# A graph layer on one core: a fixed order for VectorE's instructions in a step, and three buffers for the node columns' comparisons

## Chip, cores, metric

The kernel runs on one core of one Trainium2 chip. The metric is the device time of one execution in microseconds (us). TensorE is called PE in the profile, VectorE DVE, ScalarE ACT, GpSimd POOL; SP only issues DMAs.

## What is computed

A layer of a graph network with a residual connection and a layer norm, on 12500 nodes of 128 features and 400000 edges, sorted by target:

```python
Xs = X[src]
msg = where(edge_type == 0, Xs @ W_data.T + b_data, Xs @ W_control.T + b_control)
agg = segment_sum(msg, dst, num_segments=12500)
h = relu(agg + X @ W_self.T + b_self)
out = layernorm(x + h)
```

## The kernel before

**Groups, windows and pairs.** The 3125 chunks of 128 edges are 25 groups of 125 chunks. Since the edges are sorted by target, a chunk touches a narrow window of targets. Of each 25 chunks, 5 go one way (p) and 20 another (e). For a p chunk, GpSimd gathers the rows of the source nodes by an indirect DMA into `msg` (L825), and TensorE adds them up: `msg` is multiplied by a 0/1 matrix `psel` into a window of sums (L757). For the 20 e chunks, a *pair* (g, i), there is no gather. All x rows lie in SBUF (`x3`, in three bf16 parts). The edges of the pair are ordered by source block, and TensorE picks the source rows with a 0/1 matrix `pick` (L926, output `got`); ScalarE copies `got` to `emsg` (L940); TensorE multiplies `emsg` by a 0/1 matrix `esel` into sums (L757). There are 107 pairs and so 107 *steps*, each of which runs about 15 us. In a step w, pair w is picked, pair w+2 is ranked, pair w+3 is begun; p chunks are gathered and added on the side.

**The chain of one pair on VectorE.** `block_matrix`, `fours` and `same_lane` begin a pair: O compares each edge's source block with the 100 blocks (L533, 128x2000); `fours` adds up O's columns in groups of ten and of five (L614, L615); `same_lane` compares the edges of one lane with each other (L604). `before` multiplies by a triangular matrix on TensorE (L624). `ranks` then gives each edge its place: `ahead` (L632, reads PSUM), the product O times ahead (L636), two folds that halve the width (L641, 128x1200 and 128x600), `found` (a reduction, L643), `rank` (L645). `rank_matrix` compares ranks with 32 columns (`rm`, L533, 128x640) and multiplies with the values (`rv`, L676). `over` looks for edges whose rank is over 32 (`key` L649, `top` L653, `over_n` L660, `bits`). `put` on TensorE places the values (L688), ScalarE copies them to `cell` (L696), two DMAs on SP write them to memory and read them back to all partitions (`pick<-there`, L701), and VectorE turns them into the pick matrix (L743, in place). L709 transposes the cells on TensorE.

**The node columns' comparisons.** `choose` in `picked` builds `esel` in three parts per step: 10, 9 and 6 columns (L533 with 128x1760, 128x1584, 128x1056), traced in the turns t = 0, 1 and 3. They share two buffers.

**Spare columns.** Edges over rank 32 go through extra columns: `own_before` (L552 on TensorE, L558 `om_all` on VectorE), `own_turn` (L564), and one gather per two pairs (`both`, L901), which ScalarE copies to `last` (L988).

**Preparing a group.** `prep(g)` has four parts (`begin`, `rows`, `turn`, `then`), placed in steps at 0.15, 0.4, 0.65 and, a step later, at 0.1. `rows` works on VectorE (L494 to L499), `turn` transposes on TensorE (L504), `then` splits the indices (L511, L512, L515).

**What sets the order.** In each step, `merged` sorts lists of (position between 0 and 1, function) and calls them in that order. That is the order of tracing, not yet that of the engines: a planner then orders each engine's queue once, when the program is built, by the place in the trace and by its own estimate of when an instruction is ready. On the chip each queue runs in that order. `tc.issue_after(ins)` ties what is traced inside it behind `ins` on the same engine. `placed[0]` is the last `rv` that has been traced; `behind`, `pick_matrix` and `later` (which wraps the parts of `prep`) tie to it. The planner is free with everything else, O among it. `evenly` spreads a list over a step. `paced` gives each gather a wait for an instruction of TensorE, so that gathers follow the steps.

The steps of the loop that hold these lists, with the positions of before: `before` in turn t = 1, `ranks` 0.31, `rank_matrix` 0.35, `rows` 0.4, `begin_slots(w + 3)` 0.55, `pick_matrix(w + 1)` 0.6, `over` 0.75.

Of the kernel before, what the change touches and what calls it, by code (L numbers as in the profile page):

```python
# [8 lines left out]
FP = mybir.dt.float32  # L9
# [197 lines left out]
def short_path(ctx, tc, const, ident, eps, wT, brow, bad, x, src, dst, etype, ws, bs, out):  # L207
# [320 lines left out]

    def select(sel, col, code2):

        rows, n, width = sel.shape
        shape = [rows, n, width // 2, 2]
        nc.vector.tensor_tensor(  # L533
            sel.rearrange("p n (w t) -> p n w t", t=2),
            col[:rows].rearrange("p (o w t) -> p o w t", o=1, t=2).to_broadcast(shape),
            code2.rearrange("p n (o t) -> p n o t", o=1).to_broadcast(shape),
            op=OP.is_equal,
        )
        return sel

# [44 lines left out]
    def give_slots(w):  # L585
# [4 lines left out]

        def behind():
            return tc.issue_after(placed[0].ins) if w > 1 else ExitStack()

        def block_matrix():
            O = s["held"] = two.tile([P, EC * NCELL], BF, name="O")
            s["O"] = O.rearrange("p (c j) -> p c j", j=NCELL)
            select(s["O"], cell_cols[w % 2], blk2)

        def same_lane():
# [3 lines left out]
            with behind():  # L603
                nc.vector.tensor_tensor(  # L604
                    eq.rearrange("p a (b t) -> p a b t", t=2),
                    blk2.rearrange("p a (o t) -> p a o t", o=1).to_broadcast(shape),
                    run,
                    op=OP.is_equal,
                )
        def fours():  # L610
            s["prod"] = big.tile([P, EC, NCELL + EC], BF, name="prod")
            h = s["few"] = s["prod"][:, :, :NCELL]
            with behind():
                nc.vector.tensor_add(h[:, :2 * CQ], s["O"][:, :2 * CQ], s["O"][:, 2 * CQ:])  # L614
            nc.vector.tensor_add(h[:, 2 * CQ:3 * CQ], h[:, :CQ], h[:, CQ:2 * CQ])  # L615

# [11 lines left out]

        def ranks():
            ahead = two.tile([P, NCELL], BF, name="ahead")  # L630
            with nc.allow_low_precision(reason="whole numbers; those over 256 need not be exact"):
                nc.vector.tensor_reduce(  # L632
                    ahead, s["ahead"][:, :2 * NCELL].rearrange("p (k j) -> p j k", k=2), AX.X, OP.add
                )
            prod = s["prod"]
            nc.vector.tensor_tensor(  # L636
                prod[:, :, :NCELL], s["O"], ahead.rearrange("p (o j) -> p o j", o=1).to_broadcast([P, EC, NCELL]),
                op=OP.mult,
            )
            for h in ((NCELL + EC) // 2, (NCELL + EC) // 4):  # L640
                nc.vector.tensor_add(prod[:, :, :h], prod[:, :, :h], prod[:, :, h:2 * h])  # L641
            found = two.tile([P, EC], FP, name="found")
            nc.vector.tensor_reduce(found, prod[:, :, :h], AX.X, OP.add)  # L643
            rank = s["rank"] = two.tile([P, EC, 2], BF, name="rank")
            nc.vector.tensor_copy(rank, found.rearrange("p (c o) -> p c o", o=1).to_broadcast([P, EC, 2]))  # L645

        def over():
            key = two.tile([P, EC], FP, name="key")
            nc.vector.scalar_tensor_tensor(key, s["rank"][:, :, 0], CAP - 0.5, pk, op0=OP.is_ge, op1=OP.mult)  # L649
# [3 lines left out]
            nc.vector.max(both["top"][:, w % 2, :], key)  # L653
            if w % 2 or w == pairs - 1:
                n = w % 2 + 1
                top = both["top"][:, :n]
                full = two.tile([P, 2, 8], FP, name="full")[:, :n]
                nc.vector.tensor_scalar(full, top, 0.0, None, op0=OP.is_gt)
                with nc.allow_low_precision(reason="a whole number up to 8"):
                    nc.vector.tensor_reduce(over_n[:, w + 1 - n:w + 1], full, AX.X, OP.add)  # L660
# [11 lines left out]
        def rank_matrix():  # L672
            rm = select(big.tile([P, EC, CAP], BF, name="rm"), rank_col, s["rank"])
            rv = s["rv"] = two.tile([P, EC, 2, CAP], BF, name="rv")
            shape = [P, EC, 2, CAP // 2, 2]
            placed[:] = [nc.vector.tensor_tensor(  # L676
                rv.rearrange("p c v (r t) -> p c v r t", t=2),
                rm.rearrange("p c (o r t) -> p c o r t", o=1, t=2).to_broadcast(shape),
                vals2.rearrange("p c v (o t) -> p c v o t", o=1).to_broadcast(shape),
                op=OP.mult,  # L680
            )]

# [51 lines left out]
        return s, [(0.58, block_matrix), (0.6, fours), (0.66, same_lane)], [  # L734
            (0.1, before), (0.31, ranks), (0.35, rank_matrix), (0.75, over),
        ]

    def pick_matrix(w):

        def half(a, b):  # L740
            t = slots[w]["pick"][:, a:b].rearrange("p j r -> p (j r)")
            with tc.issue_after(placed[0].ins):
                nc.vector.tensor_scalar(t, t, lane_f, None, op0=OP.is_equal)  # L743
        return [(0.6, lambda: half(0, NCELL))]

# [99 lines left out]
    def choose(g, i):  # L845

        sel = sp.tile([P, CHUNKS, 2 * PW], BF, name="psel")
        chosen[g, i] = select(sel, near_col, codes["p", g][1][:, i * CHUNKS:(i + 1) * CHUNKS])

# [56 lines left out]
    def picked(w, tiled, ending, before):  # L906
# [7 lines left out]

        def choose(q0, n):

            sel = select(sp.tile([P, 10, 2 * EW], BF, name="esel")[:, :n], code_col, slots[w]["code"][:, q0:q0 + n])
            for k in range(n):
                s["sel"][q0 + k] = sel[:, k]

        lead = 0 if w % 2 else 2
# [30 lines left out]
        def unit(t):  # L952
# [46 lines left out]

        return evenly([lambda t=t: unit(t) for t in range(turns)]), end  # L1000

# [80 lines left out]

    begun = {}

    def last_spares():
# [13 lines left out]
    def check_all():  # L1099
# [23 lines left out]
        nc.vector.tensor_copy(bad, one_i)  # L1123

    def begin_slots(w):
        slots[w], a, b = give_slots(w)
        begun[w] = b
        return [u for _, u in a]

    def all_slots(w):  # L1130
        units = begin_slots(w) + [u for _, u in begun.pop(w)]
        units += [u for t in sorted(slots[w]["tiled"]) for u in slots[w]["tiled"][t]]
# [44 lines left out]
    for w in range(pairs):  # L1177
# [8 lines left out]
        if i == 3 and g + 2 < NG:  # L1186
            load(g + 2)
        tiled, begin = {}, []
        if w + 2 < pairs:
            tiled, begin = slots[w + 2]["tiled"], begun.pop(w + 2)  # L1190
        elif w + 2 == pairs:
            tiled, begin = last_spares()
        if w + 3 < pairs:
# [5 lines left out]
        units, ending = picked(w, tiled, ending, begin.pop(0)[1] if begin else None)  # L1199
# [161 lines left out]
```

## Time and profile before

| what | value |
|---|---|
| median of 3 runs | 1719.61 us (1719.46 to 1721.19) |
| the profiled execution | 1721.01 us |
| its span, first to last instruction | 1719.3 us |
| granted clock of TensorE | 0.994 |
| gathers, L825 and L901 | 985 of 1.234 us and 54 of 1.226 us |

The page gives busy time by engine; the table by stretches the same for chosen parts of the span; the list of waits who waited for whom, with total us, times, longest. In a timeline each line has start, duration, engine, line, operation, out<-in and shape, and in brackets the idle time before it and who ended that.

### The profile page before, as it was taken

How to read it: one execution, taken by the hardware profiler on the slowest of the kernel's cores; microseconds unless marked ns; L12 is line 12 of the kernel's file. 1: busy time of each engine (PE TensorE's matmuls, PEld its weight loads, DVE VectorE, ACT ScalarE, POOL GpSimd, SP SyncE). 2: the span in 40 equal slices, each digit the busy share in tenths (PEclk: the TensorE clock that was granted, in tenths of full speed). 3: DMA queues.
4: the chain of work that ended last, by engine and by line, in shares of the span. 5: the costliest groups of instructions: out<-in, count | busy, mean ns of one | idle time of the engine just before them, and what ended most of it. 6: DMA issues, size and time to landing. Idle time of an engine off the chain costs nothing.

```text
span 1719.3 us, 68641 instructions
## 1 busy us (share of the span) xinstructions
PE 1568.1 (91%) x28525; PEld 1241.5 (72%) x28525; DVE 1529.0 (89%) x3630; ACT 1243.3 (72%) x2198; POOL 1286.8 (75%) x1061
## 2 busy tenths in 40 slices
PE   0599999999999999999899999999999999999997
PEld 0377777777777777777677777777777777777776
DVE  6899899998998989999799899999999899999983
ACT  5777677776777667777576777676777676777675
POOL 0288878888788888888788777777788787777872
PEclk9999999999999999999999999999999999999999
DMA  7844454545444454444445554545544445544442
GB/s 195 280 149 133 126 160 124 147 147 152 134 139 142 139 148 135 140 150 129 144 122 150 160 155 136 152 130 152 150 144 138 135 128 159 155 140 129 138 128 59
DMA packets 148973, 248.30 MB, mean 144 GB/s; under 512 B 35937, under 2 KB 115260, under 8 KB 148652
## 3 DMA queue, kind: packets, MB, share of 16 engines
q1 hardware_dynamic: 85994, 134.45, 23.6%
q0 software_dynamic: 50032, 102.98, 22.2%
q10 hardware_dynamic: 12626, 6.40, 1.4%
q8 instruction: 225, 3.69, 0.9%
q14 instruction: 96, 0.79, 0.1%
HBM read 226.24 MB, written 17.50 MB: 142 GB/s over the span
## 4 chain that ended last, share of the span: by engine, by line
DVE 40%; PE 38%; issue 8%; ACT 5%; DMA 4%; DVEq 1%; POOL 0%; SPq 0%; ACTq 0%; POOLq 0%
PE sums L757 16%; PE got L926 12%; DVE esel L533 5%; DVE prod L641 5%; DVE prod L636 4%; DVE rv L676 3%; DVE pick L743 3%; DVE found L643 3%; PE side L1045 3%; ACT emsg L940 2%; DVE prod L614 2%; PE side L624 2%; DMA both<-rows,idx 2%; DVE psel L533 2%; PE side L688 2%
## 5 line engine op out<-in xcount | busy, mean ns | idle before, releaser
L825 POOL DMA_INDIRECT msg<-rows,idx_g x985 | 1215.5, 1234 | 309.7 <-issue 143.8
L940 ACT CAST emsg<-got 128x768 bf16<-128x768 f32 (+1 forms) x1070 | 949.0, 931 | 296.9 <-PE got L926 277.8
L757 PE MATMUL sums<-esel,emsg 128*128 128x176 bf16 x7704 | 686.6, 240 | 3.4 <-DVE acc L814 2.9
L757 PEld LDWEIGHTS <-emsg 128*128 128x128 bf16 x7704 | 569.5, 98 | 106.1 <-issue 98.8
L926 PE MATMUL got<-x,pick 128*32 128x384 bf16 x10486 | 569.1, 330 | 17.9 <-ACT emsg L940 8.8
L926 PEld LDWEIGHTS <-pick 128*32 128x32 bf16 x10486 | 240.4, 96 | 143.8 <-issue 19.9
L533 DVE TENSOR_TENSOR esel<-code_col,code 128x1760 bf16<-128x1760 bf16 x321 | 292.9, 913 | 11.8 <-PE sums L757 8.8
L757 PE MATMUL sums<-psel,msg 128*128 128x48 bf16 x2955 | 167.2, 184 | 11.8 <-DVE acc L814 9.0
L757 PEld LDWEIGHTS <-msg 128*128 128x128 bf16 x2955 | 138.6, 97 | 21.2 <-issue 16.4
L641 DVE TENSOR_TENSOR prod<-prod 128x1200 bf16<-128x1200 bf16 x214 | 134.0, 626 | 7.2 <-issue 1.1
L533 DVE TENSOR_TENSOR O<-cell_col,blk 128x2000 bf16<-128x2000 bf16 x107 | 128.0, 1197 | 7.1 <-ACT blk L439 4.3
L636 DVE TENSOR_TENSOR prod<-O,ahead 128x2000 bf16<-128x2000 bf16 x107 | 128.3, 1200 | 4.5 <-DVE ahead L632 1.9
L743 DVE TENSOR_SCALAR pick<-pick,lane_f 128x3200 bf16<-128x3200 bf16 x107 | 112.9, 1055 | 0.1
L901 POOL DMA_INDIRECT both<-rows,idx x54 | 66.2, 1226 | 54.4 <-ACT emsg L940 41.8
L688 PE MATMUL side<-rv,O 128*128 128x64 bf16 x2140 | 83.4, 195 | 25.0 <-DVE rv L676 22.1
L533 DVE TENSOR_TENSOR psel<-near_col,near 128x1200 bf16<-128x1200 bf16 x125 | 96.7, 773 | 9.7 <-issue 8.7
L814 DVE TENSOR_TENSOR acc<-acc,sums 128x176 f32 (+2 forms) x232 | 66.8, 288 | 42.1 <-PE sums L757 41.3
L688 PEld LDWEIGHTS <-O 128*128 128x128 bf16 x2140 | 79.0, 100 | 27.2 <-DVE rv L676 22.3
L676 DVE TENSOR_TENSOR rv<-rm,vals 128x1280 bf16<-128x1280 bf16 x107 | 87.9, 822 | 3.3 <-DVE key L649 1.4
L643 DVE TENSOR_REDUCE found<-prod 128x20 f32<-128x600 bf16 x107 | 82.9, 775 | 3.2 <-DVE prod L641 0.4
L614 DVE TENSOR_TENSOR prod<-O 128x1000 bf16<-128x1000 bf16 x107 | 72.0, 673 | 0.0
L624 PEld LDWEIGHTS <-ltri 128*128 128x128 bf16 x1284 | 40.4, 96 | 40.0 <-issue 38.5
(196 smaller groups left out, 1544.6 us busy)
## 6 DMA issues: line engine op xcount, KB each, us to landing
pick<-there SPq DMA_DIRECT2D x106, 800.0 KB
msg<-rows,idx_g POOLq DMA_INDIRECT x985
acc<-acc_start SPq DMA_DIRECT2D x23, 640.0 KB
rows<-x SPq DMA_DIRECT2D x6, 1344.0 KB
xs<-in_x_dram SPq DMA_DIRECT2D x99, 62.5 KB
out_dram<-h SPq DMA_DIRECT2D x99, 62.5 KB
xt<-in_x_dram ACTq DMA_DIRECT2D x6, 896.0 KB
cnt<-cnt_start SPq DMA_DIRECT2D x22, 160.0 KB
```

Source lines behind the costliest of these rows:

```text
L533: nc.vector.tensor_tensor(sel.rearrange("p n (w t) -> p n w t", t=2), col[:rows].rearrange("p (o w t) -> p o w t", o=1, t=2).to_broadcast( ...
L614: nc.vector.tensor_add(h[:, :2 * CQ], s["O"][:, :2 * CQ], s["O"][:, 2 * CQ:])
L636: nc.vector.tensor_tensor(prod[:, :, :NCELL], s["O"], ahead.rearrange("p (o j) -> p o j", o=1).to_broadcast([P, EC, NCELL]), op=OP.mult,)
L641: nc.vector.tensor_add(prod[:, :, :h], prod[:, :, :h], prod[:, :, h:2 * h])
L643: nc.vector.tensor_reduce(found, prod[:, :, :h], AX.X, OP.add)
L676: placed[:] = [nc.vector.tensor_tensor(rv.rearrange("p c v (r t) -> p c v r t", t=2), rm.rearrange("p c (o r t) -> p c o r t", o=1, t=2).t ...
L688: nc.tensor.matmul(s["rk"][:m, :2 * CAP], s["held"][:, c * NCELL:c * NCELL + m], s["rv"][:, c].rearrange("p v r -> p (v r)"), start=(c == ...
L743: nc.vector.tensor_scalar(t, t, lane_f, None, op0=OP.is_equal)
L757: last = nc.tensor.matmul(out, msg[:, j * D:(j + 1) * D], sel, start=(start and j == 0), stop=stop, skip_group_check=True)
L825: return nc.gpsimd.indirect_dma_start(out=msg, out_offset=None, in_=rows3[:, :], in_offset=bass.IndirectOffsetOnAxis(ap=codes["p", g][0][: ...
L926: last = nc.tensor.matmul(ps[CAP * a:CAP * (a + 1), :], slots[w]["pick"][:, a * NQ + q, :], x3[:, 4 * q + a - a0].rearrange("p j d -> p (j ...
L940: s["out"] = nc.scalar.copy(msg[:, :n], ps[:, :n, :3 * D])
```

## The change

A step's instructions on VectorE are cut into single functions, and 16 of them are put into a list, `order`, each tied behind the one before it by `issue_after` (`in_turn`). The tie starts anew in each step. The order is: second comparison of the node columns, ahead, product, first fold, third comparison, second fold, found, `same` of pair w+3, rank, rank matrix, key, values (rv), pick matrix of pair w+1, O of pair w+3, its tens, its fives. What is not in the list stays free. `over` moves from 0.75 to 0.58 and holds `key` no longer. `esel` gets three buffers, and its second and third comparison leave the turns 1 and 3 of `picked`. `begin_slots(w + 3)` at 0.503 only makes the functions. Before the loop, pick matrix 0 and the begin of pair 2 are tied behind the rv of pair 1, O included.

```diff
+    def after(ins):
+        return tc.issue_after(ins.ins) if ins is not None else ExitStack()
...
-            sel = select(sp.tile([P, 10, 2 * EW], BF, name="esel")[:, :n], code_col, slots[w]["code"][:, q0:q0 + n])
+            sel = sp.tile([P, 10, 2 * EW], BF, name="esel", bufs=3)[:, :n]
+            sel, ins = select(sel, code_col, slots[w]["code"][:, q0:q0 + n], prev)
...
-            if t == 1:
-                choose(10, 9)
-            if t == 3:
-                choose(19, NQ - 19)
...
+    def in_turn(named, prev=None):
+
+        last = [prev]
+
+        def unit(f):
+            last[0] = f(last[0])
+
+        return [lambda f=f: unit(f) for f in named]
...
-    merged(pick_matrix(0))
-    for u in begin_slots(2):
+    pick_matrix(0, placed[0])
+    for u in in_turn(begin_slots(2), placed[0]):
         u()
...
-            tiled, begin = slots[w + 2]["tiled"], begun.pop(w + 2)
+            tiled, first, chain = slots[w + 2]["tiled"], slots[w + 2]["before"], slots[w + 2]["chain"]
+            begin = [(0.58, slots[w + 2]["over"])]
...
-            more += [(0.55, lambda: [u() for u in begin_slots(w + 3)])]
+            more += [(0.503, lambda: begin_slots(w + 3))]
...
+        order = [
+            (0.305, second), (0.31, chain.get("ahead")), (0.33, chain.get("product")), (0.34, chain.get("half")),
+            (0.36, third), (0.38, chain.get("fourth")),
+            (0.52, chain.get("found")), (0.53, started("same")), (0.54, chain.get("rank")),
+            (0.55, chain.get("matrix")), (0.56, chain.get("key")), (0.57, chain.get("values")),
+            (0.6, (lambda prev: pick_matrix(w + 1, prev)) if w + 1 < pairs else None),
+            (0.62, started("blocks")), (0.64, started("tens")), (0.66, started("fives")),
+        ]
+        order = [(at, f) for at, f in order if f]
+        order = [(at, u) for (at, _), u in zip(order, in_turn([f for _, f in order]))]
         merged(
             chunks.pop(w, []),
             units,
             begin,
-            pick_matrix(w + 1) if w + 1 < pairs else [],
+            order,
             more,
             evenly(rest, 0.1),
         )
```

More of the change, by code (lines that the diff above doesn't have):

```diff
@@ L627, in before, with ahead @@
                     )
[L629 to L633, printed above, removed]
-                )
-            prod = s["prod"]
[L636 to L645, printed above, removed]
+        def ahead(prev=None):
+            s["ahead_b"] = two.tile([P, NCELL], BF, name="ahead")
+            with nc.allow_low_precision(reason="whole numbers; those over 256 need not be exact"), after(prev):
+                return nc.vector.tensor_reduce(
+                    s["ahead_b"], s["ahead"][:, :2 * NCELL].rearrange("p (k j) -> p j k", k=2), AX.X, OP.add
+                )
@@ new lines, in product, with fold, found @@
+        def product(prev=None):
+            with after(prev):
+                return nc.vector.tensor_tensor(
+                    s["prod"][:, :, :NCELL], s["O"],
+                    s["ahead_b"].rearrange("p (o j) -> p o j", o=1).to_broadcast([P, EC, NCELL]), op=OP.mult,
+                )
+        def fold(h, prev=None):
+            prod = s["prod"]
+            with after(prev):
+                return nc.vector.tensor_add(prod[:, :, :h], prod[:, :, :h], prod[:, :, h:2 * h])
+        def found(prev=None):
+            s["found"] = two.tile([P, EC], FP, name="found")
+            with after(prev):
+                return nc.vector.tensor_reduce(s["found"], s["prod"][:, :, :(NCELL + EC) // 4], AX.X, OP.add)
@@ new lines, in rank, with key @@
+        def rank(prev=None):
+            s["rank"] = two.tile([P, EC, 2], BF, name="rank")
+            with after(prev):
+                return nc.vector.tensor_copy(
+                    s["rank"], s["found"].rearrange("p (c o) -> p c o", o=1).to_broadcast([P, EC, 2])
+                )
+        def key(prev=None):
+            s["key"] = two.tile([P, EC], FP, name="key")
+            with after(prev):
+                return nc.vector.scalar_tensor_tensor(
+                    s["key"], s["rank"][:, :, 0], CAP - 0.5, pk, op0=OP.is_ge, op1=OP.mult
+                )
@@ L733, in give_slots, with pick_matrix @@
             s["own_turn"] = own_turn
[L734 to L744, printed above, removed]
+        wide = NCELL + EC
+        s["begin"] = {"blocks": block_matrix, "same": same_lane, "tens": tens, "fives": fives}
+        s["chain"] = {
+            "ahead": ahead, "product": product, "half": lambda prev=None: fold(wide // 2, prev),
+            "fourth": lambda prev=None: fold(wide // 4, prev), "found": found, "rank": rank,
+            "matrix": rank_matrix, "key": key, "values": values,
+        }
+        s["before"], s["over"] = before, over
+        return s
+    def pick_matrix(w, prev):
+        t = slots[w]["pick"].rearrange("p j r -> p (j r)")
+        with after(prev):
+            return nc.vector.tensor_scalar(t, t, lane_f, None, op0=OP.is_equal)
     acc, added, parts_in = {}, [], {}
```

90 lines of the change are left out of this document (49 added, 41 removed).

## The prediction

> **What bounds the kernel now.** I read the page's busy times first, then the table by stretches, then the list of waits, then the timeline of two steps. The page:
>
> ```profile
> PE 1568.1 (91%) x28525; PEld 1241.5 (72%) x28525; DVE 1529.0 (89%) x3630; ACT 1243.3 (72%) x2198; POOL 1286.8 (75%) x1061
> ```
>
> Two engines are near 90%, so the average decides nothing. The stretches (length, then busy time of PE, PEld, DVE, ACT, POOL, each with its count, then granted clock and DMA) do:
>
> ```profile
> core 0: us, PE busy (x) PEld busy (x) DVE busy (x) ACT busy (x) POOL busy (x), PEclk, DMA share, GB/s
> 200.00:1600.00 1400.00, 1324.59 (x24259) 1051.33 (x24263) 1270.63 (x2969) 1023.09 (x1841) 1110.89 (x902) 0.99 0.47 142
> ...
> 860.50:875.60 15.10, 14.02 (x259) 10.72 (x257) 13.90 (x37) 11.73 (x26) 12.36 (x10) 1.00 0.40 121
> 1240.70:1253.20 12.50, 12.50 (x241) 9.95 (x239) 11.36 (x20) 9.99 (x15) 10.06 (x9) 1.00 0.47 152
> ```
>
> The last row is a step that carries nothing besides its own work: TensorE is busy for 12.50 of 12.50 us, VectorE has 1.14 us to spare. No order of VectorE's work can shorten such a step. The row above it is a step in which a group's codes are also prepared: TensorE is idle for 1.08 us. Over the middle 1400 us TensorE is idle for 75.4 us; that, 5.4%, is all that a better order could win there. The waits say who ends this idle time (total us, times, longest):
>
> ```profile
> ACT last L988 <- DMA both<-rows,idx: 29.0, 16, 7.1
> ...
> PE side L709 <- ACT cell L696: 27.2, 14, 6.3
> ...
> PE side L504 <- DVE code_r L496: 11.9, 18, 1.1
> ...
> DVE esel L533 <- PE sums L757: 8.8, 20, 2.1
> ...
> PE got L926 <- DVE pick L743: 8.1, 17, 1.0
> ...
> PE side L564 <- DVE om_all L558: 6.4, 21, 0.7
> ...
> PE side L552 <- DVE over_n L660: 4.1, 7, 0.9
> ```
>
> VectorE is late for TensorE in four places: the codes' transposes (L504), the pick matrix (L743), the spare columns' matrix (L558) and their number (L660): 11.9 + 8.1 + 6.4 + 4.1 = 30.5 us. TensorE never waits for the node columns' comparisons (no row of TensorE names esel); it is VectorE that waits for TensorE there, 8.8 us. So the third buffer by itself takes away waits of an engine that has time.
>
> **A third party: GpSimd.** Its 902 spans in the middle 1400 us take 1110.89 us. The timeline shows what stands between them:
>
> ```profile
> 823.64 0.95 POOL L825 DMA_INDIRECT msg<-rows,idx_g  x1 [0.30 <-issue]
> ...
> 812.42 0.82 DVE L676 TENSOR_TENSOR rv<-rm,vals 128x1280 bf16<-128x1280 bf16 x1
> 812.89 1.18 POOL L825 DMA_INDIRECT msg<-rows,idx_g  x1 [0.31 <-DMA msg<-rows,idx_g]
> 813.17 0.67 DVE L614 TENSOR_TENSOR prod<-O 128x1000 bf16<-128x1000 bf16 x1
> ```
>
> 0.30 us precede each gather, whatever it waits for: 1110.89 + 902 x 0.30 = 1381.5 us, so 18.5 of 1400 us are spare, about 21 us over the some 1600 us behind the prologue. The gathers follow TensorE at nearly the rate that GpSimd can give. If TensorE gains more than that, the gather of the spare columns' rows (both) comes later, and ScalarE's copy behind it (L988) holds the cells that TensorE waits for at L709. So this is a lid on any gain, unless the gathers themselves get shorter.
>
> **The change part by part.** The preparing step above, in order of time:
>
> ```profile
> 863.02 0.78 DVE L643 TENSOR_REDUCE found<-prod 128x20 f32<-128x600 bf16 x1
> ...
> 863.83 0.19 DVE L645 CAST rank<-found 128x40 bf16<-128x40 f32 x1
> 864.05 0.49 DVE L533 TENSOR_TENSOR rm<-rank_col,rank 128x640 bf16<-128x640 bf16 x1
> ...
> 864.46 0.70 DVE L533 TENSOR_TENSOR esel<-code_col,code 128x1056 bf16<-128x1056 bf16 x1
> 865.08 0.82 DVE L676 TENSOR_TENSOR rv<-rm,vals 128x1280 bf16<-128x1280 bf16 x1
> ...
> 865.82 0.48 DVE L494 TENSOR_SCALAR rel<-dsts,near_all 125x128 bf16<-125x128 int32 x2
> ...
> 866.95 0.33 PE L504 MATMUL side<-ident,code_r 125*128 125x125 f32 x1 [0.88 <-DVE code_r L496]
> ...
> 867.21 0.68 DVE L614 TENSOR_TENSOR prod<-O 128x1000 bf16<-128x1000 bf16 x1
> ...
> 867.80 0.37 DVE L604 TENSOR_TENSOR prod<-blk,blk 128x400 bf16<-128x400 bf16 x1
> ...
> 868.09 0.42 DVE L615 TENSOR_TENSOR prod<-prod 128x500 bf16<-128x500 bf16 x1
> 868.42 1.05 DVE L743 TENSOR_SCALAR pick<-pick,lane_f 128x3200 bf16<-128x3200 bf16 x1
> ...
> 869.60 0.77 PE L688 MATMUL side<-rv,O 128*128 128x64 bf16 x20
> ...
> 870.44 1.00 PE L926 MATMUL got<-x,pick 128*32 128x384 bf16 x20
> ...
> 871.58 1.20 DVE L533 TENSOR_TENSOR O<-cell_col,blk 128x2000 bf16<-128x2000 bf16 x1
> 872.69 0.40 DVE L558 TENSOR_SCALAR om_all<-slot_col,side 128x70 bf16<-128x70 bf16 x2
> ...
> 873.15 0.53 PE L564 MATMUL side<-bits_b,om_all 128*128 128x3 bf16 x14 [0.20 <-DVE om_all L558]
> ```
>
> *The holes.* An instruction that reads its forerunner's result starts 0.03 us after that one's end (863.02 + 0.78 = 863.80, next 863.83); a foreign one starts 0.08 us before it (864.05 + 0.49 = 864.54, next 864.46). A filled hole is worth 0.11 us. The new order fills two per step, the third comparison between the two folds and the lane comparison (L604) between found and rank. It opens two: O, its tens and its fives, each reading the one before, now stand in a row. Between rm and rv a foreign instruction stood already. Net: 2 x 0.11 - 2 x 0.11 = 0 us per step on VectorE. The title's foreign operations bring nothing by themselves; position does.
>
> *The pick matrix.* Now L614, L604 and L615 stand between rv and L743: from 867.21 to 868.42, 1.21 us. After the change L743 follows rv (or the few instructions of 0.1 us on the overflowing edges, `over`, that are traced just ahead of it, some 0.6 us in every other step). Of the three only L604 now precedes rv: 0.29 us (from its start to the next). So the pick matrix ends about 0.9 us sooner in a plain step, and 17 waits of 8.1 us in all, longest 1.0, go: -7 us. Its data must have landed:
>
> ```profile
> 1238.28 0.34 SPq L701 DMA_DIRECT2D pick<-there  x1
> ...
> 1245.28 0.82 DVE L676 TENSOR_TENSOR rv<-rm,vals 128x1280 bf16<-128x1280 bf16 x1
> ...
> 1247.22 1.05 DVE L743 TENSOR_SCALAR pick<-pick,lane_f 128x3200 bf16<-128x3200 bf16 x1
> ...
> 1247.95 0.76 PE L688 MATMUL side<-rv,O 128*128 128x64 bf16 x20
> ...
> 1675.35 0.34 SPq L701 DMA_DIRECT2D pick<-there  x1
> ...
> 1679.88 1.05 DVE L743 TENSOR_SCALAR pick<-pick,lane_f 128x3200 bf16<-128x3200 bf16 x1
> ```
>
> In the plain step 8.9 us lie between its issue and its use; near the end 4.5 us were enough. One or two us sooner still finds it there: 0 us.
>
> *The preparing rows (L494 to L499).* They are queued behind the last rv that has been traced. Traced at 0.4, they now find rv at 0.35 of the same step; in the new order rv is traced at 0.57, so they hang on the rv of the step before and may run ahead of found. Their 1.39 us (865.82 to 867.21) leave the gap between rv and pick, and the codes are there when L504 wants them: of 11.9 us I take -9. In return rv moves back by 1.39 + 0.29. In the step shown rv ends at 865.90 and L688 starts at 869.60: 3.70 us, less the 0.88 that L504 no longer waits, 2.8 us; 1.7 us fit. Where the third comparison stood behind rv, 0.62 us come on top; still inside. I book +2 us for the few steps in which a window's addition also falls in there.
>
> *O, tens and fives.* O now runs just ahead of om_all; in the new order it is done before the next step begins. Its 1.11 us (871.58 to 872.69) leave the path to L564, and `over`, traced at 0.58 and not at 0.75, brings over_n forward. Of 6.4 + 4.1 us I take -6. For nothing: lower bound 0, where the planner puts another comparison into the same place; upper bound 10.5.
>
> *Third buffer, second comparison ahead of the counts.* Cover: VectorE's own idle time; 0 us. If VectorE were the last to arrive, it would be the 8.8 us.
>
> *Before the steps.* The O of pair 2 can no longer slide into the prologue's gaps; it is queued behind rv of pair 1, together with what follows it. Bounds 0 and its 1.20 us: +1 us.
>
> *The lid.* -7 - 9 - 6 + 2 + 1 = -19 us. That is nearly the whole of the 21 us that GpSimd has to spare, and the lag is not the same everywhere: more waits of the kind of L988, now 29.0 us, of which TensorE sees most at L709. Between 0 and the whole gain I take +5. Sum: -14 us. The profiled execution took 1721.0 us (span 1719.3), 1.4 above the median of 1719.6; against that median I forecast 1706 us.
>
> *A rule against it.* The Trainium skill (SBUF — State Buffer, Who interferes with whom) says that a VectorE instruction with two SBUF inputs contends with a GpSimd instruction that reads SBUF, and that the loser blocks fully. By that rule, filled holes would keep gathers out longer. The rows of 812.42 show blocking, but only for one instruction: the gather ends at 814.07, 0.83 after rv's end, although the tens (two inputs as well) had started 0.07 us before that end. So it was let in between two overlapping instructions.
>
> **The rivals.**
> *(B) GpSimd's lid takes it all.* TensorE's waits for VectorE vanish, those at L709 grow by the same amount. For it: only 18.5 us spare in 1400. Against it: that is still a full percent. Time: 1717 to 1722.
> *(C) Gathers get longer.* The first of the two folds is this group of the table by lines (count, busy us, mean ns, idle before):
>
> ```profile
> L641 DVE TENSOR_TENSOR prod<-prod 128x1200 bf16<-128x1200 bf16 x107 | 83.8, 783 | 4.3 <-issue 1.1 <-DVE prod L636 0.5
> ```
>
> A gather that asks during its 0.78 us now would wait through the third comparison (0.62 us from start to next) and the second, half as long fold, together 1.0 us more. 902 gathers and 1400 us give 0.64 per us, so 0.5 of them per step, and 107 steps 53 us, less 21 spare: about +32, 1750 us. It decides from 0.02 us per gather on (18.5 us over 902). Against it: the row at 812.89. The rule above would have it so.
> *(D) rv becomes late; slower.* Everything put ahead of rv (L604, third, the rows, windows' additions that now find no other room) delays L688, and behind it cell, the bounce through memory and the next pick. In the plain step rv ends at 1246.10 and L688 starts at 1247.95: 1.85 us; it decides from there on. If rv moves back by 2.2 us in all of some 105 steps, 0.35 x 105 = 37 us, less the 22 gained: 1736 us. For it: the order is fixed, so a long foreign instruction can no longer be passed by one of the chain's. Against it: in the plain step only 0.3 to 0.4 us are added.
> *(E) The lid lifts.* Smoother steps also remove half of L709's 27.2 us and the +5: about 1687 us.
>
> **How the numbers follow.** Forecast 0.48 (own range 1694 to 1715), E 0.08, B 0.14, C 0.08, D 0.22. A measurement of this kernel can tell about 0.2%, 3.4 us: 1716.2 to 1723.0 counts as no change. Faster: 0.48 + 0.08 + 0.02 of B = 0.58; within 0.2%: 0.12; slower: C and D, 0.30. The range runs from 1688 (E's edge) to 1732 (most of D); C, the rest of D and half of E are left out, about 0.2.
>
> **What would show it.** Right: the row L926 waiting for pick gone from the waits, L504 for code_r under 4 us, L564 for om_all under 3; DVE order rv, pick, O, tens, fives; VectorE's busy sum unchanged; TensorE's idle time in the middle near 60 us; GpSimd's spare time down to a few us. Wrong: a new row of L688 waiting for rv (D), gathers above 1.26 us on average (C), L709 and L988 above 35 us (B), or L743 waiting for its DMA.

## The result, and the profile after

The changed kernel takes 1709.83 us (median of 6 runs, 1706.58 to 1714.88), the kernel before, on the same chip, 1719.53 us: a ratio of 0.9939, interval 0.9921 to 0.9958. Ratios here and below are of fast runs alone and differ a little from the quotients of the medians. The forecast was 1706 us. The profiled execution took 1708.33 us. Its page, then its stretch of 200 to 1600 us (columns as before):

```profile
span 1706.6 us, 68558 instructions
...
PE 1560.1 (91%) x28525; PEld 1239.0 (73%) x28525; DVE 1515.2 (89%) x3630; ACT 1244.3 (73%) x2198; POOL 1265.2 (74%) x1061
...
DVE 56%; PE 23%; issue 8%; DMA 5%; ACT 4%; DVEq 2%; SPq 0%; POOL 0%; ACTq 0%; POOLq 0%
```

```profile
200.00:1600.00 1400.00, 1331.85 (x24491) 1060.55 (x24490) 1274.19 (x3004) 1030.99 (x1859) 1103.81 (x907) 1.00 0.48 143
```

TensorE's idle time in the middle fell from 75.4 to 68.2 us, GpSimd's busy time from 1286.8 to 1265.2 us in the whole span. Over the whole span TensorE was busy for 8.0 us less and idle for 4.7 us less (146.5 and not 151.2). VectorE's share of the chain that ended last is now 56% (40% before, by the same part of that page). The waits that answer to those shown before, with the additions' (`acc`) row of the kernel before first, which the prediction doesn't list:

```profile
PE sums L757 <- DVE acc L814: 12.0, 19, 1.1
```

```profile
PE sums L789 <- DVE acc L846: 26.5, 45, 1.7
PE side L738 <- ACT cell L725: 24.9, 33, 5.8
...
PE side L568 <- DVE om_all L562: 10.9, 21, 1.5
ACT last L1018 <- DMA both<-rows,idx: 9.3, 10, 1.7
...
PE side L556 <- DVE over_n L684: 5.2, 11, 2.4
...
PE got L960 <- DVE pick L776: 1.4, 4, 0.6
```

The wait of L504 for code_r (11.9 us) has no row any more, and the wait for the pick fell from 8.1 to 1.4 us. In their place the additions (`acc`) are late for TensorE: 26.5 us in 45 waits, 12.0 in 19 before. om_all rose from 6.4 to 10.9, over_n from 4.1 to 5.2 us. The copy to `last` waits 9.3 us and not 29.0. One step's timeline shows the new order, and why the additions are late:

```profile
848.71 0.82 DVE L704 TENSOR_TENSOR rv<-rm,vals 128x1280 bf16<-128x1280 bf16 x1
849.18 1.52 POOL L857 DMA_INDIRECT msg<-rows,idx_g  x1 [0.30 <-issue]
849.45 0.18 DVE L677 MAX8 top<-key 128x8 f32<-128x20 f32 x1
849.54 1.04 DVE L776 TENSOR_SCALAR pick<-pick,lane_f 128x3200 bf16<-128x3200 bf16 x1
...
850.65 1.19 DVE L537 TENSOR_TENSOR O<-cell_col,blk 128x2000 bf16<-128x2000 bf16 x1
...
852.07 0.67 DVE L616 TENSOR_TENSOR prod<-O 128x1000 bf16<-128x1000 bf16 x1
...
853.45 0.97 DVE L537 TENSOR_TENSOR esel<-code_col,code 128x1584 bf16<-128x1584 bf16 x1
854.35 0.40 DVE L562 TENSOR_SCALAR om_all<-slot_col,side 128x70 bf16<-128x70 bf16 x2
...
854.65 0.33 DVE L846 TENSOR_TENSOR acc<-acc,sums 128x176 f32 x1
854.79 0.51 PE L568 MATMUL side<-bits_b,om_all 128*128 128x3 bf16 x14 [0.51 <-DVE om_all L562]
```

rv, top, pick, O, tens and the second comparison run in a row; om_all and acc come behind them all.

**Where the time may have come from.** A place to look is GpSimd. Its first gather starts at 76 to 77 us in both kernels, its last one ends 23 us before the end of the span. In between lie 1039 gathers, each with 0.30 us ahead of it (312 us). Taken from the trace, gather by gather:

| kernel | span, us | all gathers (msg and both), us | left on GpSimd between first and last, us |
|---|---|---|---|
| before | 1719.3 | 1281.7 | 27.0 |
| changed | 1706.6 | 1259.8 | 35.9 |
| over late | 1719.1 | 1242.8 | 66.0 |
| three buffers alone | 1744.2 | 1302.7 | 31.5 |
| pick first | 1721.0 | 1286.7 | 23.4 |
| rows early alone | 1707.6 | 1267.3 | 27.5 |
| rows and over early | 1735.6 | 1293.7 | 28.3 |

Apart from one kernel, GpSimd has 23 to 36 us to spare whatever the span is, and the span goes with the length of the gathers, though not one for one. For the change: gathers -21.9 us, spare time +8.9, together -13.0; the span fell by 12.7. For the rows alone (an experiment below): gathers -14.4, span -11.7, while TensorE's idle time did not fall (151.9 us). This is an account of one engine's time and not a path that the profile shows: the chain that ended last has 0% of POOL. The two rows of the table by lines:

```profile
L825 POOL DMA_INDIRECT msg<-rows,idx_g x985 | 1215.5, 1234 | 309.7 <-issue 143.8 <-PE got L926 61.5 <-PE sums L757 56.0
```

```profile
L857 POOL DMA_INDIRECT msg<-rows,idx_g x985 | 1193.3, 1211 | 314.8 <-issue 121.3 <-PE got L960 72.6 <-PE sums L789 63.7
```

The same 985 gathers, 23 ns shorter each. Which ones, the timeline of before tells, in the preparing step that the prediction goes through (its L614 and L743 are the instructions left out here):

```profile
866.81 0.29 DVE L497 SCALAR_TENSOR_TENSOR code_r<-kind_r,rel 125x128 f32<-125x128 f32 x1
...
867.01 0.29 DVE L499 TENSOR_TENSOR worst<-worst,rel 125x256 bf16<-125x256 bf16 x1
867.03 2.56 POOL L825 DMA_INDIRECT msg<-rows,idx_g  x1 [0.30 <-issue]
```

This gather ends at 869.59, 0.12 us after the pick's end (868.42 + 1.05 = 869.47). It asked 0.02 us into the last of the preparing rows, and was held up while that row, tens, lane comparison, fives and pick ran; at which of their boundaries it got on, the trace doesn't say. In before there are 16 such gathers, 2.56 us on average, 41.0 us together; without anything in the way a gather takes 0.95. The changed kernel has the rows elsewhere:

```profile
584.09 0.28 DVE L497 SCALAR_TENSOR_TENSOR code_r<-kind_r,rel 125x128 f32<-125x128 f32 x1
584.26 0.94 POOL L857 DMA_INDIRECT msg<-rows,idx_g  x1 [0.31 <-PE side L630]
584.29 0.29 DVE L499 TENSOR_TENSOR worst<-worst,rel 125x256 bf16<-125x256 bf16 x1
```

This one takes 0.94 us, but it is not the same request: it asks during L497, 0.03 us ahead of the last row. The like for like is in the kernel *pick first* (below), where the request comes 0.01 to 0.02 us into the same row and the pick follows at once:

```profile
870.06 0.29 DVE L499 TENSOR_TENSOR worst<-worst,rel 125x256 bf16<-125x256 bf16 x1
870.07 1.35 POOL L825 DMA_INDIRECT msg<-rows,idx_g  x1 [0.30 <-issue]
870.26 1.05 DVE L743 TENSOR_SCALAR pick<-pick,lane_f 128x3200 bf16<-128x3200 bf16 x1
```

It too ends 0.11 us after the pick, but the pick comes sooner: 1.35 us and not 2.56. Gathers of over 2 us: 49 in before, 17 after. The fixed order holds gathers up at a place of its own: 68 of the 71 that ask during rv end 0.12 us after the pick's end, 1.54 us each, as the one at 849.18 above; it is milder, since rv and pick stand together. In before, 66 of the 73 that ask during rv end 0.82 us after rv's end (or 0.95 after they asked, where that is later), as the prediction's 812.89 did. By that measure the gather of 849.18 would have ended at 850.35, while the pick ran (849.54 to 850.58). So these rows can be read as a gather that gets in at rv's end and whose last part the pick holds up; that reading was not tried by itself, and it does not fit the 16 of the kind at 867.03.

### The profile page after: what moved, and what is told of

It is laid out like the page before. It is cut to its first block, busy times and chain, and to the rows that moved or that the text cites. A ratio compares the mean times of both kernels' runs of the same rounds, so it can differ in the third digit from the quotient of the medians.

```text
span 1706.6 us, 68558 instructions
## 1 busy us (share of the span) xinstructions
PE 1560.1 (91%) x28525; PEld 1239.0 (73%) x28525; DVE 1515.2 (89%) x3630; ACT 1244.3 (73%) x2198; POOL 1265.2 (74%) x1061
## 4 chain that ended last, share of the span: by engine, by line
DVE 56%; PE 23%; issue 8%; DMA 5%; ACT 4%; DVEq 2%; SPq 0%; POOL 0%; ACTq 0%; POOLq 0%
PE sums L789 10%; DVE esel L537 8%; PE got L960 7%; DVE O L537 6%; DVE prod L652 6%; DVE prod L644 5%; DVE pick L776 5%; DVE rv L704 4%; DVE prod L616 3%; DVE found L657 2%; DVE psel L537 2%; DVE rm L537 2%; DVEq L840 2%; DVE ahead L638 2%; DVE prod L606 2%
## 5 line engine op out<-in xcount | busy, mean ns | idle before, releaser
L857 POOL DMA_INDIRECT msg<-rows,idx_g x985 | 1193.3, 1211 | 314.8 <-issue 121.3
L960 PE MATMUL got<-x,pick 128*32 128x384 bf16 x10486 | 565.6, 330 | 9.7 <-ACT emsg L974 6.0
L960 PEld LDWEIGHTS <-pick 128*32 128x32 bf16 x10486 | 239.6, 96 | 136.8 <-issue 21.8
L537 DVE TENSOR_TENSOR esel<-code_col,code 128x1760 bf16<-128x1760 bf16 x321 | 296.7, 924 | 21.1 <-issue 10.9
L717 PE MATMUL side<-rv,O 128*128 128x64 bf16 x2140 | 82.8, 195 | 25.4 <-DVE rv L704 22.4
L717 PEld LDWEIGHTS <-O 128*128 128x128 bf16 x2140 | 78.8, 100 | 28.6 <-DVE rv L704 21.8
L638 DVE TENSOR_REDUCE ahead<-side 128x100 bf16<-128x200 f32 x107 | 38.7, 362 | 66.9 <-PE side L630 63.0
```

Source lines behind the costliest of these rows:

```text
L537: ins = nc.vector.tensor_tensor(sel.rearrange("p n (w t) -> p n w t", t=2), col[:rows].rearrange("p (o w t) -> p o w t", o=1, t=2).to_broa ...
L717: nc.tensor.matmul(s["rk"][:m, :2 * CAP], s["held"][:, c * NCELL:c * NCELL + m], s["rv"][:, c].rearrange("p v r -> p (v r)"), start=(c == ...
L857: return nc.gpsimd.indirect_dma_start(out=msg, out_offset=None, in_=rows3[:, :], in_offset=bass.IndirectOffsetOnAxis(ap=codes["p", g][0][: ...
L960: last = nc.tensor.matmul(ps[CAP * a:CAP * (a + 1), :], slots[w]["pick"][:, a * NQ + q, :], x3[:, 4 * q + a - a0].rearrange("p j d -> p (j ...
```

## The experiments

Each ratio is against the kernel before on the same chip.

**over late** (changed kernel)

```diff
-            begin = [(0.58, slots[w + 2]["over"])]
+            begin = [(0.75, slots[w + 2]["over"])]
```

> The changed kernel, with the overflow work (over) traced at 0.75 again and not at 0.58. My theory: at 0.58 ScalarE's bits_b stands in its queue ahead of the cells' copy and holds it (bits_b waits 47.7 us in the changed kernel, 18.8 before; TensorE's L738 then waits 24.9 us in short pieces). At 0.75 it falls behind again: bits_b under 25 us, L738 under 15 us, 1702 to 1707 us. Rival: over early is needed for om_all (10.9 us): over_n and om_all waits grow by 5 us or more, 1712 to 1718 us.

1720.94 us, 0.9992 (0.9979 to 1.0005): the whole gain is gone. The signs that the theory named came (bits_b 24.0 us, L738 9.1), its time did not.

```profile
PE side L556 <- DVE over_n L684: 36.5, 35, 2.4
PE sums L789 <- DVE acc L846: 28.1, 42, 1.9
ACT bits_b L694 <- DVE bits L692: 24.0, 32, 3.3
...
PE side L738 <- ACT cell L725: 9.1, 8, 5.8
```

In the fixed order, `over` at its old place falls behind O, tens and fives, and TensorE waits 36.5 us for over_n (5.2 before the edit). The gathers are the shortest of all in the table, 1242.8 us, and GpSimd has 66 us to spare: shorter gathers bring nothing where TensorE waits for VectorE this long. So `over` early is a condition of the fixed order, not a gain over the kernel before.

**Three buffers alone** (kernel before)

```diff
-            sel = select(sp.tile([P, 10, 2 * EW], BF, name="esel")[:, :n], code_col, slots[w]["code"][:, q0:q0 + n])
+            sel = select(sp.tile([P, 10, 2 * EW], BF, name="esel", bufs=3)[:, :n], code_col, slots[w]["code"][:, q0:q0 + n])
```

> The kernel before, with three buffers for esel and nothing else. My theory: TensorE never waited for esel, so 1716 to 1723 us, no change. Rival (the buffers bring the gain, since VectorE's work can then be moved ahead): 1709 to 1713 us and additions' waits of 26 us as in the changed kernel.

1745.09 us, 1.0118 (1.0091 to 1.0145), which neither expectation had. The buffer was to take a wait away from VectorE, an engine that had time. That wait fell only from 8.8 to 6.7 us, and the kernel became slower by 1.2%.

```profile
L825 POOL DMA_INDIRECT msg<-rows,idx_g x985 | 1235.4, 1254 | 314.3 <-issue 133.8 <-PE sums L757 71.2 <-PE got L926 60.6
```

```profile
PE side L709 <- ACT cell L696: 35.7, 29, 5.7
...
PE got L926 <- DVE pick L743: 16.0, 21, 1.4
```

The msg gathers are 20 us longer, and of all gathers 62 take over 2 us (49 before); TensorE waits twice as long for the pick (8.1 us before). That the planner now puts comparisons where the queue had gaps is the likely way; it was not tried apart.

**Pick first** (kernel before): lane comparison, tens and fives tied behind the pick matrix and not behind rv.

```diff
-            return tc.issue_after(placed[0].ins) if w > 1 else ExitStack()
+            return tc.issue_after(picked_last[0].ins) if w > 1 else ExitStack()
...
-                nc.vector.tensor_scalar(t, t, lane_f, None, op0=OP.is_equal)
+                picked_last[:] = [nc.vector.tensor_scalar(t, t, lane_f, None, op0=OP.is_equal)]
...
-            more += [(0.55, lambda: [u() for u in begin_slots(w + 3)])]
+            more += [(0.605, lambda: [u() for u in begin_slots(w + 3)])]
```

> The kernel before, with one move: the tens, fives and lane comparison of the next pair are tied behind the pick matrix and not behind rv, so that the pick matrix follows rv. My theory: TensorE's wait for pick falls from 8.1 us to under 2, 1711 to 1716 us. Rival (the lid of GpSimd): the waits vanish, L709 grows by as much, 1717 to 1722 us.

1719.34 us, 0.9987 (0.9973 to 1.0001): nothing that can be told. The wait for the pick is gone, and it came back elsewhere:

```profile
ACT last L988 <- DMA both<-rows,idx: 34.6, 18, 5.4
PE side L709 <- ACT cell L696: 32.5, 20, 5.7
```

```profile
L825 POOL DMA_INDIRECT msg<-rows,idx_g x985 | 1215.3, 1234 | 305.0 <-issue 137.1 <-PE got L926 56.5 <-PE sums L757 54.1
```

The 16 gathers that ask during the last row now take 1.35 us each, 19 us less, but gathers at other places became longer by as much: the 38 that ask during the pick take 2.19 us each (39 of 1.23 us before). With the msg gathers unchanged in sum, the time is unchanged, and the waits moved to the cell and the copy to `last`, as the rival with the lid had it.

**Rows early alone** (kernel before)

```diff
-            prepared = [(at, lambda u=u: later(u)) for at, u in zip((0.15, 0.4, 0.65, 0.1), prep(g + 1))]
+            prepared = [(at, lambda u=u: later(u)) for at, u in zip((0.15, 0.3, 0.65, 0.1), prep(g + 1))]
```

> The kernel before, with one move: the preparing rows are traced at 0.3 and not at 0.4, so that they hang on the rv of the step before and may run ahead of the chain. My theory: L504's wait for code_r falls from 11.9 us to under 3, that for pick by some 3 as well, 1708 to 1715 us. Rival (rv becomes late): L688 waits for rv instead, 5 to 10 us, 1717 to 1723 us.

1706.11 us, 0.9899 (0.9877 to 0.9921). One number, 0.4 to 0.3, makes the rows hang on the rv of the step before, as the whole change does, and gives at least as much as the whole change (the two intervals touch). It is a little better than the theory's 1708 to 1715.

```profile
L825 POOL DMA_INDIRECT msg<-rows,idx_g x985 | 1201.5, 1220 | 311.9 <-issue 129.5 <-PE got L926 72.3 <-PE sums L757 60.4
```

```profile
PE side L709 <- ACT cell L696: 32.8, 27, 5.7
...
PE side L564 <- DVE om_all L558: 10.0, 15, 1.3
```

No row of L504 for code_r, no gather held up from the rows to the pick; 14 us less of gathers, span 11.7 us shorter. TensorE's 11.9 us for code_r came back as other waits: the cell rose from 27.2 to 32.8, om_all from 6.4 to 10.0, and the sum of its idle time stayed (151.9 us, 151.2 before).

**Another kind of chip.** The next seven kernels ran on two chips on which the kernel before takes 1996.56 and 1995.13 us. Single instructions take about as long there (L926 334 ns, 330 before), and the gathers together no longer; but TensorE waits for its own instructions. Weight loads of L960 in the changed kernel, on the first chip and on one of these; then a piece of the latter's timeline:

```profile
PEld L960 <- issue: 21.8, 71, 2.5
```

```profile
PEld L960 <- issue: 190.7, 368, 2.4
```

```profile
300.73 0.19 PEld L630 LDWEIGHTS <-ltri 128*128 128x128 bf16 x5 [0.53 <-issue]
301.22 0.18 PEld L630 LDWEIGHTS <-ltri 128*128 128x128 bf16 x4 [0.30 <-issue]
301.95 0.14 PEld L630 LDWEIGHTS <-ltri 128*128 128x128 bf16 x3 [0.55 <-issue]
```

Three to five weight loads, then half a microsecond of nothing that the profile shows. In the changed kernel GpSimd has 344 us to spare there, so these chips show the edits without the lid.

**Rows late** in the changed kernel, and three more on one such chip:

```diff
-            prepared = [(at, lambda u=u: later(u)) for at, u in zip((0.15, 0.4, 0.65, 0.1), prep(g + 1))]
+            prepared = [(at, lambda u=u: later(u)) for at, u in zip((0.15, 0.575, 0.65, 0.1), prep(g + 1))]
```

> The changed kernel, with the preparing rows traced at 0.575 and not at 0.4, so that they hang on the same step's rv again and stand between rv and pick as before the change. Theory (the rows' place is nearly the whole gain; it was worth 13 us alone in the kernel before): 1709.8 + 13 = about 1722 us, TensorE waits for code_r for 8 us or more again, the sum of the other waits about as in the changed kernel. Rival (the fixed order brings the gain by itself, and the rows' place would have been worth the same as any one of its parts): 1708 to 1713 us. Between them, 1716: each has half.

2006.40 us, 1.0049 (1.0030 to 1.0068), with a wait of 4.0 us for code_r. The numbers expected were for the first chip; the edit is taken up again below.

**Two buffers in the fixed order** (changed kernel, `name="esel", bufs=3` becomes `name="esel"`)

> The changed kernel with two buffers for the node columns' comparisons, the order kept. Theory (the third buffer lets comparisons run early, ahead of what TensorE waits for; it cost 20 us alone in the kernel before, and in the fixed order most of them are tied, so less is to be had back): 1700 to 1706 us, the waits for acc (26.5 us) and om_all (10.9 us) lower. Rival (in the fixed order the second comparison stands ahead of the counts and needs its buffer free; with two it waits for the additions' matmuls and holds all of the chain behind it): above 1715 us, with a row of VectorE's esel waiting for TensorE's sums far above the few us of now.

2008.98 us, 1.0058 (1.0035 to 1.0080), against 1.0022 (1.0004 to 1.0041) for the changed kernel on the other such chip; the intervals just overlap. The wait that the rival named is there: the second comparison needs its buffer early. VectorE's wait, changed kernel first:

```profile
DVE esel L537 <- PE sums L789: 24.5, 17, 3.9
```

```profile
DVE esel L537 <- PE sums L789: 104.1, 83, 3.5
```

So the third buffer costs alone (on the first chip) and takes a long wait away in the fixed order, where all of the chain is tied behind that comparison.

**Rows early and pick first** (kernel before, both edits)

> The kernel before with two edits together: the preparing rows traced at 0.3, and the pick matrix right behind rv. Theory (the picks' 8 us come back as waits for the cell and the spare columns' copy as long as GpSimd is the lid): 1704 to 1708 us, as with the rows alone (1706.1), no wait for pick, L709 above 28 us. Rival (with the rows out of the way the picks' own waits are worth their size): 1698 to 1702 us.

1992.80 us, 0.9972 (0.9951 to 0.9993), no better than the rows alone (0.9941, 0.9918 to 0.9964, on the other such chip). The pick's own place shows no gain here either.

**The order without its ties** (changed kernel)

```diff
-        order = [(at, u) for (at, _), u in zip(order, in_turn([f for _, f in order]))]
+        order = [(at, u) for (at, _), u in zip(order, untied([(f, at in (0.53, 0.6, 0.64, 0.66)) for at, f in order]))]
```

`untied` gives each function `placed[0]` where the second entry is true, and no tie otherwise.

> The changed kernel, with its trace positions and three buffers, but with the ties of the order taken off: only the lane comparison, tens, fives and pick hang on the last rv traced. Theory (the ties cost: the window's additions and the spare columns' matrix queue behind comparisons, tens and fives, 26.5 and 10.9 us of waits): 1703 to 1707 us, with both waits lower. Rival (the ties hold VectorE's chain in order, and untied, with three buffers, comparisons run ahead of it as they did in the kernel before with three buffers alone): 1715 to 1740 us.

1992.89 us, 0.9989 (0.9968 to 1.0009). Against the changed kernel on the other such chip the wait for acc is lower, as the theory had it (9.0 against 19.0 us), that for om_all is not (9.6 against 4.8). The intervals of 0.9989 and 1.0022 touch, so a cost of the ties is likely and not shown.

**Four cases on one chip** (again one of the second kind): changed kernel, the same with the rows late (as above), and the kernel before with the rows early (as above).

> The changed kernel itself, beside the next two, so that the four cases (old and new order of VectorE, rows late and early) stand on one chip. On a chip as the first: ratio to the kernel before 0.992 to 0.996. On a chip as the last one, where TensorE waits for its own instructions for over 100 us: between 0.995 and 1.003.

> The changed kernel with the preparing rows traced at 0.575, behind the same step's rv as before the change. Theory (the rows' place is the gain): 0.7% above the changed kernel and 0.2% or more above the kernel before, with waits for code_r of 8 us or more again. Rival (the fixed order has a gain of its own of some 5 us or more): below the kernel before by 0.3% or more.

> The kernel before with the preparing rows traced at 0.3 alone. Theory: at least as fast as the changed kernel, ratio to before 0.988 to 0.993 on a chip as the first; where TensorE's own instructions are late, a smaller gain, 0.994 to 0.998. Rival (the earlier run of this edit was an accident of the planner and of that chip): within 0.2% of the kernel before on a chip as the last one, while the changed kernel is faster there.

| | rows late | rows early |
|---|---|---|
| order of before | 1995.13 us (1) | 1981.53 us, 0.9941 (0.9918 to 0.9964) |
| fixed order | 2006.14 us, 1.0053 (1.0033 to 1.0073) | 1998.88 us, 1.0022 (1.0004 to 1.0041) |

Read across, moving the rows gives 0.6% in the old order and about 0.3% in the new one (the intervals of the lower line just overlap). Read down, all the rest of the change costs 0.5 to 0.8%. On this kind of chip the whole change is no gain (0.2% slower). The rival of the second run (a gain of the fixed order by itself) is refuted here; its theory has the sign, but the move was worth 0.3% and not 0.7%, and the wait for code_r, known from the other such chip alone, was 4.0 us and not 8. The rows' place as the source of the gain holds in both lines.

This bears on the reading by gathers. With the rows early the kernel before has 323.9 us to spare on GpSimd on this chip, and still the move brings 0.6% (1.0% on the first chip). So gathers that are short by some microseconds can't be why it pays here. The program is the same on both chips, so this run speaks against an accident of the chip, not against one of the planner's order. TensorE's wait for code_r is the way that is left; no trace of the kernel before was taken on these chips to show it, and no run tells on the first chip how much each of the two gave.

**Rows early and over early** (kernel before)

```diff
-        return s, [(0.58, block_matrix), (0.6, fours), (0.66, same_lane)], [
-            (0.1, before), (0.31, ranks), (0.35, rank_matrix), (0.75, over),
+        return s, [(0.58, block_matrix), (0.6, fours), (0.66, same_lane)], [
+            (0.1, before), (0.31, ranks), (0.35, rank_matrix), (0.58, over),
```

> The kernel before with two edits: the preparing rows traced at 0.3, and over traced at 0.58 and not at 0.75, as the changed kernel has it. Theory (over early takes the waits for over_n and om_all, the term of 6 us in the prediction, and nothing else is late for it): 0.2 to 0.4% below the rows alone, so a ratio to before of 0.985 to 0.988 on the first chip, of 0.989 to 0.992 on the later two. Rival (over's instructions now stand between rv and the pick matrix, and the waits go to the pick or to the cell): the ratio of the rows alone or above it, 0.990 to 0.995 on the first chip, 0.994 to 0.998 on the later two, with om_all's wait no lower than 4 us.

On a chip like the first (before: 1721.45 us) 1739.65 us, 1.0117 (1.0094 to 1.0140). Neither expectation: 2.2% above the rows alone.

```profile
285.62 0.81 DVE L676 TENSOR_TENSOR rv<-rm,vals 128x1280 bf16<-128x1280 bf16 x1
285.90 2.90 POOL L901 DMA_INDIRECT both<-rows,idx  x1 [0.30 <-DMA msg<-rows,idx_g]
...
287.56 0.17 DVE L653 MAX8 top<-key 128x8 f32<-128x20 f32 x1
287.65 1.03 DVE L743 TENSOR_SCALAR pick<-pick,lane_f 128x3200 bf16<-128x3200 bf16 x1
```

```profile
L825 POOL DMA_INDIRECT msg<-rows,idx_g x985 | 1220.5, 1239 | 310.9 <-issue 128.9 <-PE got L926 63.2 <-PE sums L757 59.4
```

```profile
ACT last L988 <- DMA both<-rows,idx: 59.1, 24, 7.3
PE side L709 <- ACT cell L696: 54.7, 28, 6.2
```

`top`, 0.17 us long, now stands between fives and pick, and VectorE is never idle from rv to the pick's end: the gather takes 2.90 us, to 0.12 us behind it. 24 gathers take over 2.5 us (11 with the rows alone), of which four stand like this one, all gathers together 26 us more, and the chain by `both`, `last` and the cell passes it on to TensorE. That `top` alone does this was not tried; `key`, `full`, `over_n` and `bits` moved too.

## Why the prediction was right, and where it was not

**The sum** was -14 us against the profiled execution; it measured -12.7. The sum and its sign are right; of the reasons, half. That the size came out is in part luck: the -7 and the -6 did not come as time, and the gathers' -21.9 us were not in the sum.

**Preparing rows, -9:** right in place and size: TensorE's wait went (11.9 us to none), and rows early alone, on two kinds of chip, shows that the rows' place brings the gain. Whether it does so by that wait is open, since on the first chip the wait came back elsewhere. The same move also ended the 2.56 us gathers, which the prediction didn't see, though the row at 867.03 stands between rows that it quotes.

**Pick matrix, -7:** TensorE's wait did go (8.1 to 1.4), and pick first shows no gain from that alone.

**O and over, -6:** wrong in sign. om_all and over_n went from 10.5 to 16.1 us. The step that failed is that O's 1.11 us "leave the path to L564": O left, but tens and the second comparison came to stand there. The prediction had named this case, at 0 and not at a loss. And its list of four places where VectorE is late leaves out the additions, 12.0 us, more than any of the four; acc came to stand behind the same instructions, 14.5 us more.

**rv later, +2, and before the steps, +1:** small, as booked: of TensorE's wait for rv, now 22.4 us, all but 0.7 lies before the steps, as it did in the kernel before (22.1).

**The third buffer, 0:** 0 in a sum, but not by the cover named. VectorE's idle time doesn't make it free: alone it costs 1.2%, in the fixed order its absence costs.

**The lid, +5:** the prediction had GpSimd as a lid on TensorE's gain, "unless the gathers themselves get shorter", which it named and then left. They did, by 21.9 us; the span fell by 12.7. On the first chip the runs fit a GpSimd that is nearly always full, a closer bound than a lid worth 5 us; over late, with gathers shorter by 38.9 us and no gain, and the chips where GpSimd has over 300 us to spare show that it is not the only one. Rival C (a filled hole keeps gathers out) was looked for in the wrong place, the two folds, and with the wrong sign for this change; its outcome, longer gathers, is what three buffers alone and rows with over early ran into. The signs named for it (gathers above 1.26 us on average) were the right ones to look at, though none reaches that size: 1.254 and 1.239 us of msg in those two kernels, 1.234 before, 1.211 and 1.220 in the changed kernel and with the rows early.

The rule cited there, of the Trainium skill (SBUF — State Buffer, Who interferes with whom), blocks the loser until the other's instruction ends. The prediction's reading of 812.89 (let in between two overlapping instructions) fits the 66 of 73 above. The gather of 867.03 was not let in at the end of the row during which it asked; one of 17 such was, and took 1.09 us. So neither that rule for one instruction nor the prediction's reading covers it. What decides whether a gather gets in at a boundary stays open; no run changed the gathers and nothing else.

**The signs.** Right: code_r under 4 us, pick gone, the order, VectorE's busy time nearly (1529.0 to 1515.2). Wrong: om_all under 3, TensorE's idle time near 60 (68.2), GpSimd's spare time down to a few us (it rose from 27.0 to 35.9).

**The version that beats both** is the kernel before with the rows early: 0.9899 on the first chip, where the change gave 0.9939 (the intervals touch), and 0.9941 on the second kind, where the change gave 1.0022 (they are apart).

## What to carry to other kernels

Add up busy time and the fixed time ahead of each instruction for every engine, from its first work to its last: an engine that shows 75% can have next to nothing to spare, as GpSimd here. If that engine is GpSimd with gathers, look for the gathers that are longer than the shortest, and for the run of VectorE's instructions that kept them out; moving a few small instructions brought the gain here, though both the gathers and a wait of TensorE went with them, and both a third buffer alone and an earlier `over` made the kernel 1.2% slower. Before you call such an engine the bound, look for a run in which it has time to spare. And do the parts of a large change one at a time: here one position in a list was the gain, and the rest cost some of it.

## What was not expected of the hardware

How long a gather takes can depend on what VectorE runs next: asked 0.02 us into the same row, 16 took 2.56 us each where four instructions followed up to the pick's end, 16 took 1.35 us where the pick came at once. And chips differ: on two of them the kernel before took 16% longer (1995 against 1720 us), with nearly equal durations of single instructions and TensorE waiting for its own instructions (190.7 against 21.8 us at one line's weight loads); why, no run shows. The granted clock was lower there (0.979 against 0.997 for the changed kernel), but by its records the stretches at 0.5 lost 43.0 us against 6.4, of a difference of 290. On the first chip too the clock has a part: stretches at 0.5 lost 12.0 us before and 6.4 after, at most 5.6 of the 8.0 us by which TensorE's busy time fell (1568.1 to 1560.1 us). All but the last stretch of each begin during, or within 2 us after, an idle time of TensorE of 1.5 to 6.3 us, but idle times as long stand elsewhere with no such stretch by them (1.69 us at 1284.4 in the changed kernel).
